# Four graph layers on one core: the first layer's pair loop takes its product of two row vectors from TensorE, and its epilogue no longer forms u

## The chip, the core and the metric

The kernel runs on one core of a Trainium2 chip. It computes four graph layers over 4096 nodes with 128 features each, in float32, in one launch. The metric is the device time of the launch in microseconds (us). Before the change it is 2199.0 us, the median of three runs (2198.42 to 2199.36).

An engine is named as the profile names it: PE is TensorE (PEld its weight loads), DVE is VectorE, ACT is ScalarE, POOL is GpSimd, SP is the queue that issues most transfers.

## The reference, cut to what matters

Only the first of the four layers is touched. For each node it makes a point h in the unit ball, and then sums, over the neighbours j of a node i, the logarithmic map of h_j seen from h_i, weighted by a sigmoid:

```python
        h = proj(mobius_add(mv, hyp_bias))                   # one 128-vector a node, |h| < 1
        x_tangent = logmap0(h)
        x_local = jax.vmap(lambda xi: logmap(xi, h))(h)      # for all 4096 x 4096 pairs
        logits = (x_tangent @ wl)[:, None] + (x_tangent @ wr)[None, :] + att_b[0]
        adj_att = adj * jax.nn.sigmoid(logits)
        support_t = jnp.einsum('ij,ijd->id', adj_att, x_local)
        h_agg = proj(expmap(h, support_t))
        out = proj(expmap0(proj_tan0(h_agg)))
        ...
    x = _layernorm(x + _L0_gnn_ref(x, adj, ...), axis=-1)
```

`logmap` is a multiple of a Moebius sum of the two points, times an inverse hyperbolic tangent of its norm. The kernel never forms it for a pair. With g = h / (1 - |h|^2) and e = sqrt(|g|^2 + 1/4) for each node, everything that a pair (i, j) needs is the scalar

    t = e_i * e_j - g_i . g_j

clamped from below just above 1/4, and a function phi(t) = ln(2 (2t + s)) / s with s = sqrt(4 t^2 - 1/4). The sums over j are then matrix products of (sigmoid x adj x phi) with g.

## The kernel before: the parts that the change and the steps touch

After a preamble that makes `H` (the g of all nodes, by rows), `HT` (the same, transposed), `gg` = |g|^2, `ex` = e, and the vectors of the sigmoid (`dl`, `dr`), comes the *pair loop*. It goes over the 36 pairs (I, J), I <= J, of the 8 x 8 blocks of 512 x 512 nodes. An off-diagonal pair does block (I, J) and block (J, I) at once (t is symmetric: the second one takes a transpose); 28 pairs are off-diagonal and 8 diagonal. Before the loop the rows e and dl are written to DRAM and read back, spread over all partitions:

```python
            ex = de[:, 1, :]
            nc.vector.tensor_scalar(ex, gg, 0.25, None, op0=ALU.add)
            nc.scalar.activation(ex, ex, AF.Sqrt)
            ...
            nc.tensor.transpose(p[0 : 2 * NT, 0, :], de.rearrange("p k t -> p (k t)"), self.ident)
            nc.scalar.copy(e2, p[0 : 2 * NT, 0, :])
            nc.sync.dma_start(out=rows.rearrange("k (t p) -> (k t) p", p=P), in_=e2)
```

The loop's operations, each for one pair `p` (and one block `m`, `b` or `ib` of 128 rows):

```python
            def load(p, k):                       # SP: broadcasts (di, ei or dj) and a 1 MB block of adj
                ...
                        row["d", I] = broadcast(0, I, "di")
                        row["e", I] = broadcast(1, I, "ei")
                ...
            def turn_adj(p, m):                   # PE: transposes a 128-row strip of adj into PSUM (2 buffers)
            def copy(p, m, put=nc.scalar.copy):   # ACT: takes it from PSUM into at
            def vcopy(p, m):                      # DVE: the same
            def store(p, k):                      # SP: writes the transposed block for the later layers, 1 MB
            def distance(p, b):                   # PE: pz = g_j . g_i for 128 x 512 pairs (PSUM, 2 buffers)
                nc.tensor.matmul(
                    pz, lhsT=HT[:, j * P : (j + 1) * P], rhs=HT[:, I * S : (I + 1) * S], start=True, stop=True
                )
            def shift(p, b):                      # DVE: t = e_i * e_j - pz
                nc.vector.scalar_tensor_tensor(
                    once(p, "t", wk, "t")[:, b, :], st[p]["e"], ex[:, j : j + 1], st[p].pop(("pz", b)),
                    op0=ALU.mult, op1=ALU.subtract,
                )
            def sigmoid(p, k):                    # ACT: 4 x sigmoid(d + dr), 128 x 512 each
            def mask(p, k):                       # DVE: w = w * at
            def clamp(p, _):                      # DVE: y = max(t, 0.25 + 5e-7)
                nc.vector.tensor_scalar(y, st[p]["t"], 0.25 + 5e-7, None, op0=ALU.max)
            def square(p, _):                     # ACT; then ln, root, inverse: ACT, all 128 x 2048
            def add_root(p, _):                   # DVE: t = 2 t + s
            def log(p, _):                        # ACT
            def phi(p, _):                        # DVE: t = t * y
            def first(p, _):                      # DVE: w0 = w0 * t
            def turn(p, ib):                      # PE: transposes t (the same 2 PSUM buffers as distance)
            def second(p, ib):                    # DVE: w1 = w1 * transposed t
            # sum_i, sum_j: PE, the two matrix products; add_j, add_i: DVE, adding them up in XA
```

The order of all these within a step is one string, `PAIR_ORDER`; the last number of an entry says how many pairs ahead of the step it works. An engine takes its instructions strictly in this order:

```python
PAIR_ORDER = """
turn_adj.4.0 first.0.-1 copy.4.0 distance.2.1 second.3.-1 mask.0.0 ln.0.0 turn_adj.1.1 turn.1.-1
root.0.0 sum_i.1.-2 turn_adj.0.1 shift.2.1 copy.1.1 copy.0.1 mask.1.0 load.1.1 add_i.0.-2 add_root.0.0
store.1.0 sum_j.0.-2 distance.1.1 turn_adj.3.1 turn_adj.5.1 inverse.0.0 sum_i.0.-1 second.1.-1
add_j.0.-2 distance.0.1 log.0.0 shift.1.1 sigmoid.0.1 vcopy.3.1 distance.3.1 turn_adj.2.1 add_j.1.-2
vcopy.5.1 sum_i.3.-1 phi.0.0 shift.0.1 load.0.2 turn_adj.7.1 sum_i.2.-1 copy.2.1 turn.2.0 shift.3.1
clamp.0.1 turn.0.0 turn_adj.6.1 vcopy.7.1 sigmoid.1.1 second.2.0 copy.6.1 second.0.0 square.0.1
sum_j.1.-1 store.0.1 turn.3.0
"""
```

The *epilogue* follows. `X` holds the weighted sums v of the 32 groups of 128 nodes. It forms u = bhalf v + sm g in place and sums its squares (`uu`), then w = sg u + b g and its squares (`wsq`), then c2 w + c1 b g and its squares (`gsq`), each a pass over 32 tiles of 128 x 128, with a few small column operations and activation-table loads between; then the residual and the layer norm, whose tiles go straight into the second layer:

```python
            for t in range(NT):
                nc.gpsimd.tensor_scalar(Hb[:, t, :], H[:, t, :], b[:, t : t + 1], None, op0=ALU.mult)
            for t in range(NT):
                nc.vector.scalar_tensor_tensor(           # gv = g . v
                    junk, H[:, t, :], 1.0, X[:, t, :], op0=ALU.mult, op1=ALU.mult, accum_out=gv[:, t : t + 1]
                )
                nc.scalar.activation(X[:, t, :], X[:, t, :], AF.Copy, scale=bhalf[:, t : t + 1])
            ...
            for t in range(NT):
                combine(t, sm, H, X, uu, 2)               # DVE: X = H * sm + X; its square on DVE or ACT
            un = self.norm("un", uu)
            th = self.act("sg", self.tt("unb", un, rb, ALU.mult), AF.Tanh)
            sg = self.tt("sgu", th, self.rec("run", un), ALU.mult)
            for t in range(NT):
                combine(t, sg, X, Hb, wsq, 2)             # DVE: X = X * sg + Hb; its square
            ...
            for t in range(NT):                           # Hb = Hb * c1, on POOL or ACT
                ...
            for t in range(NT):
                combine(t, c2, X, Hb, gsq, 3)             # DVE: X = X * c2 + Hb; its square
```

Of the kernel before, what the change touches and what calls it, by code (L numbers as in the profile page):

```python
# [9 lines left out]
F32 = mybir.dt.float32  # L10
# [22 lines left out]
turn_adj.4.0 first.0.-1 copy.4.0 distance.2.1 second.3.-1 mask.0.0 ln.0.0 turn_adj.1.1 turn.1.-1  # L33
root.0.0 sum_i.1.-2 turn_adj.0.1 shift.2.1 copy.1.1 copy.0.1 mask.1.0 load.1.1 add_i.0.-2 add_root.0.0
store.1.0 sum_j.0.-2 distance.1.1 turn_adj.3.1 turn_adj.5.1 inverse.0.0 sum_i.0.-1 second.1.-1
add_j.0.-2 distance.0.1 log.0.0 shift.1.1 sigmoid.0.1 vcopy.3.1 distance.3.1 turn_adj.2.1 add_j.1.-2
vcopy.5.1 sum_i.3.-1 phi.0.0 shift.0.1 load.0.2 turn_adj.7.1 sum_i.2.-1 copy.2.1 turn.2.0 shift.3.1
clamp.0.1 turn.0.0 turn_adj.6.1 vcopy.7.1 sigmoid.1.1 second.2.0 copy.6.1 second.0.0 square.0.1
sum_j.1.-1 store.0.1 turn.3.0
# [3 lines left out]
class Net:  # L43
# [234 lines left out]
    def layer0(self, x, weight, bias, att_w, att_b):  # L278
# [4 lines left out]
        with ExitStack() as ctx:  # L283
# [122 lines left out]
            de = self.cols.tile([P, 2, NT], F32, tag="de", name="de")  # L406
# [15 lines left out]
            ex = de[:, 1, :]  # L422
# [3 lines left out]
            nc.vector.reciprocal(b, rb)  # L426

# [7 lines left out]
            rows = self.dram.tile([2, N], F32, tag="rows", name="rows")  # L435
            p = self.ps_t.tile([P, 4, P], F32, tag="pt", name="pt")
            nc.tensor.transpose(p[0 : 2 * NT, 0, :], de.rearrange("p k t -> p (k t)"), self.ident)
            e2 = pre.tile([2 * NT, P], F32, tag="e2", name="e2")
            nc.scalar.copy(e2, p[0 : 2 * NT, 0, :])
            nc.sync.dma_start(out=rows.rearrange("k (t p) -> (k t) p", p=P), in_=e2)  # L440
# [8 lines left out]
            self.pair_loop(HT, HA, dr, ex, rows, adp, early)  # L449
# [5 lines left out]
            rot = ctx.enter_context(tc.tile_pool(name="rot0", bufs=4))  # L455
            Hb = late.tile([P, NT, D], F32, tag="Hb", name="Hb")
            gv = self.col("gv")
            for t in range(NT):
                nc.gpsimd.tensor_scalar(Hb[:, t, :], H[:, t, :], b[:, t : t + 1], None, op0=ALU.mult)
            for t in range(NT):  # L460
                junk = rot.tile([P, P], F32, tag="junk", name="junk")
                nc.vector.scalar_tensor_tensor(
                    junk, H[:, t, :], 1.0, X[:, t, :], op0=ALU.mult, op1=ALU.mult, accum_out=gv[:, t : t + 1]
                )
                nc.scalar.activation(X[:, t, :], X[:, t, :], AF.Copy, scale=bhalf[:, t : t + 1])
# [4 lines left out]
            def combine(t, a, src, add, sq, of_eight):  # L470

                k = slice(t, t + 1)
                junk = rot.tile([P, P], F32, tag="junk", name="junk")
                x = X[:, t, :]
                nc.vector.scalar_tensor_tensor(x, src[:, t, :], a[:, k], add[:, t, :], op0=ALU.mult, op1=ALU.add)
                if t * of_eight % 8 < of_eight:
                    nc.vector.scalar_tensor_tensor(
                        junk, x, 1.0, x, op0=ALU.mult, op1=ALU.mult, accum_out=sq[:, k]
                    )
                else:  # L480
                    nc.scalar.activation(junk, x, AF.Square, accum_out=sq[:, k])

            uu, wsq, gsq = self.col("uu"), self.col("wsq"), self.col("gsq")
            for t in range(NT):
                combine(t, sm, H, X, uu, 2)


            un = self.norm("un", uu)
            th = self.act("sg", self.tt("unb", un, rb, ALU.mult), AF.Tanh)
            sg = self.tt("sgu", th, self.rec("run", un), ALU.mult)  # L490
            for t in range(NT):
                combine(t, sg, X, Hb, wsq, 2)
# [8 lines left out]
            c1 = self.tt("c1", rden, wsq, ALU.mult)  # L501
            for t in range(NT):
                if t % 2:
                    nc.gpsimd.tensor_scalar(Hb[:, t, :], Hb[:, t, :], c1[:, t : t + 1], None, op0=ALU.mult)
                else:
                    nc.scalar.activation(Hb[:, t, :], Hb[:, t, :], AF.Copy, scale=c1[:, t : t + 1])
            for t in range(NT):
                combine(t, c2, X, Hb, gsq, 3)
# [10 lines left out]
            for t in range(NT):  # L519
                nc.vector.scalar_tensor_tensor(  # L520
                    X[:, t, :], X[:, t, :], gf[:, t : t + 1], x0[:, t, :], op0=ALU.mult, op1=ALU.add
# [4 lines left out]
    def pair_loop(self, HT, HA, dr, ex, rows, adp, early):  # L526
# [6 lines left out]
        with ExitStack() as ctx:  # L533
# [10 lines left out]
            row = {}  # L544
# [6 lines left out]
            def broadcast(k, I, tag):  # L551

                t = wk.tile([P, S], F32, tag=tag, name=tag)
# [9 lines left out]
            def load(p, k):  # L563
                I, J = pairs[p]
                if k == 0:
                    if I == J:
                        row["d", I] = broadcast(0, I, "di")
                        row["e", I] = broadcast(1, I, "ei")
                    else:
                        row["d", J] = broadcast(0, J, "dj")  # L570
                    st[p]["d"] = [row["d", i] for i, _ in sides(p)]
                    st[p]["e"] = row["e", I]
# [988 lines left out]
```

## Time and profile before

| stretch of the span (2194.8 us) | from - to, us | what it is |
|---|---|---|
| preamble | 0 - 71 | g, e and the sigmoid's vectors |
| pair loop | 71 - 766 | 36 pairs |
| epilogue of the first layer | 766 - about 842 | three passes, layer norm; the second layer's first products start at 842 |
| the other three layers | to 2194.8 | not touched |

The page gives the busy share of each engine over the whole span: PE 88%, DVE 86%, ACT 67%, POOL 4%. These are averages over stages with different limits, so the stages that the change touches are read for themselves. A stretch in the "windows" view has one column for each engine (busy us, and in brackets the number of instructions), then the granted TensorE clock, the mean busy share of the 16 transfer engines and the GB/s they moved. In the "lines" view a row is a group of instructions of one line of the kernel: engine, operation, output <- inputs, shape, count, then busy us in all and the mean ns of one, then how long the engine had been idle before them and for whom it waited. Consecutive instructions of one engine overlap a little in these records (the next one starts before the last one's record ends), so the sum of the means of a step is a little more than the step; the distance from one start to the next is the better cost where instructions follow each other without a wait.

### The profile page before, as it was taken

Reading aid. Unit: us, or ns where it says so; the run is one execution under the profiler, and the core shown is the slowest. Engines: PE = TensorE matmul, PEld = TensorE weight load, DVE = VectorE, ACT = ScalarE, POOL = GpSimd, SP = SyncE. Lnnn points to the kernel's source line nnn. Section 1 sums busy time; section 2 is a strip of 40 time slices with the busy share of each in tenths; the row PEclk is TensorE's granted clock in tenths of the full one; section 3 lists DMA queues with packets and bytes.
Section 4 is the critical chain, followed back from the end, with each engine's and each line's share of the span. In section 5 each row is a group of like instructions: output and inputs, shape, how many; then the busy total and the mean of one; then the engine's idle time right before and its main releaser. Section 6 shows DMA issues by size and latency. Waiting matters only on the chain.

```text
span 2194.8 us, 24059 instructions
## 1 busy us (share of the span) xinstructions
PE 1936.8 (88%) x8720; PEld 1043.1 (48%) x8720; DVE 1880.6 (86%) x2732; ACT 1474.8 (67%) x1858; POOL 97.8 (4%) x146
## 2 busy tenths in 40 slices
PE   5588888888888707999999999999997999999998
PEld 4366666666666604433333333333333444544443
DVE  6799999999999888789999999999998454568887
ACT  5799999999999774677787787787784122210000
POOL 2000000000000232210000000000000000000000
PEclk7699999999999957999999999999999999999999
DMA  3456566766666406994646465564554877767783
GB/s 94 138 205 232 199 229 211 244 211 229 208 204 211 147 1 223 227 241 166 198 173 186 159 194 185 181 189 173 174 207 187 318 267 269 267 249 278 292 297 112
DMA packets 112868, 448.44 MB, mean 204 GB/s; under 512 B 9760, under 2 KB 20064, under 8 KB 71776
## 3 DMA queue, kind: packets, MB, share of 16 engines
q1 hardware_dynamic: 94160, 361.82, 46.8%
q10 hardware_dynamic: 9360, 68.16, 9.1%
q0 software_dynamic: 9216, 16.78, 4.3%
q8 instruction: 73, 1.20, 0.2%
q14 instruction: 59, 0.48, 0.1%
HBM read 369.10 MB, written 77.63 MB: 204 GB/s over the span
## 4 chain that ended last, share of the span: by engine, by line
PE 41%; DVE 35%; ACT 17%; issue 5%; DMA 2%; POOL 0%; ACTq 0%; SPq 0%; DVEq 0%; POOLq 0%
PE pa L1264 10%; PE pv L926 9%; DVE e L909 9%; PE pa L1444 9%; PE ps L900 6%; ACT e L907 4%; DVE w L620 4%; ACT w L612 3%; DVE t L603 2%; DVE nat L890 2%; DVE w L652 2%; DVE t L648 2%; DVE w L663 2%; DVE at L584 1%; DVE t L640 1%
## 5 line engine op out<-in xcount | busy, mean ns | idle before, releaser
L909 DVE SCALAR_TENSOR_TENSOR e<-at,e 128x2048 f32<-128x2048 f32 x256 | 582.8, 2286 | 69.5 <-ACT e L907 68.9
L907 ACT ACTIVATE e<-ps 128x1024 f32<-128x1024 f32 x512 | 493.1, 1024 | 146.2 <-PE ps L900 126.3
L926 PE MATMUL pv<-e,VA 128*64 128x512 f32 x2048 | 495.8, 605 | 6.6 <-DVE e L909 4.9
L900 PE MATMUL ps<-QS,KS 128*128 128x512 f32 x1024 | 313.4, 425 | 4.9 <-ACT e L907 2.6
L900 PEld LDWEIGHTS ps<-QS,KS 128*128 128x128 f32 x1024 | 171.7, 189 | 229.5 <-ACT e L907 174.4
L926 PEld LDWEIGHTS pv<-e,VA 128*64 128x64 f32 x2048 | 124.6, 136 | 249.4 <-issue 215.1
L1264 PE MATMUL pa<-ring,Y 128*128 128x512 f32 x512 | 225.7, 594 | 0.0
L580 PE MATMUL ptA<-ident,ad 128*128 128x128 f32 x1024 | 159.5, 285 | 51.6 <-ACT at L584 48.1
L1444 PE MATMUL pa<-w,F 128*128 128x512 f32 x448 | 195.3, 594 | 0.0
L580 PEld LDWEIGHTS ptA<-ident,ad 128*128 128x128 f32 x1024 | 120.7, 145 | 132.5 <-ACT at L584 95.8
L1441 DVE SCALAR_TENSOR_TENSOR w<-rho,col,ring 128x512 f32<-128x512 f32 x224 | 162.7, 745 | 22.9 <-PE pa L1444 10.3
L596 PE MATMUL pz<-HT 128*128 128x512 f32 x288 | 152.8, 633 | 23.3 <-DVE w L663 16.2
L675 PE MATMUL pi<-HA,w 128*128 128x129 f32 x1152 | 153.6, 278 | 0.6 <-DVE w L652 0.6
L1264 PEld LDWEIGHTS pa<-ring,Y 128*128 128x128 f32 x512 | 95.9, 191 | 111.5 <-issue 111.3
L620 DVE TENSOR_TENSOR w<-w,at 128x2048 f32<-128x2048 f32 x64 | 146.0, 2282 | 0.5 <-ACT at L584 0.5
L675 PEld LDWEIGHTS pi<-HA,w 128*128 128x128 f32 x1152 | 141.4, 194 | 3.8 <-issue 2.3
L1444 PEld LDWEIGHTS pa<-w,F 128*128 128x128 f32 x448 | 83.7, 190 | 106.1 <-issue 78.3
L881 ACT ACTIVATE nat<-nat 128x2048 f32<-128x2048 f32 x64 | 122.6, 1916 | 3.7 <-DMA nat<-in_adj_dram 3.6
L690 PE MATMUL pj<-HA,w 128*128 128x129 f32 x896 | 109.5, 274 | 3.0 <-DVE w L663 3.0
L603 DVE SCALAR_TENSOR_TENSOR t<-ei,de,pz 128x512 f32<-128x512 f32 x144 | 103.6, 738 | 9.5 <-DMA ei<-rows 7.0
L690 PEld LDWEIGHTS pj<-HA,w 128*128 128x128 f32 x896 | 104.5, 191 | 3.2 <-DVE w L663 3.2
L658 PE MATMUL ptz<-ident,t 128*128 128x128 f32 x448 | 70.0, 282 | 33.8 <-DVE w L663 24.7
(359 smaller groups left out, 2446.5 us busy)
## 6 DMA issues: line engine op xcount, KB each, us to landing
ring<-adjT SPq DMA_DIRECT2D x128, 1024.0 KB, 4.8
ad<-in_adj_dram SPq DMA_DIRECT2D x64, 1024.0 KB, 5.3
adjT<-at SPq DMA_DIRECT2D x64, 1024.0 KB, 5.0
nat<-in_adj_dram ACTq DMA_DIRECT2D x64, 1024.0 KB, 5.0
at<-adjT SPq DMA_DIRECT2D x63, 1024.0 KB, 4.8
qk<-cut SPq DMA_DIRECT2D x16, 512.0 KB, 12.1
KS<-qk POOLq DMA_DIRECT2D x32, 256.0 KB, 7.4
QS<-qk POOLq DMA_DIRECT2D x32, 256.0 KB, 5.6
```

What stands on the lines that cost most here:

```text
L580: nc.tensor.transpose(pt[:, ib, :], ad[:, ib, jb * P : (jb + 1) * P], self.ident)
L596: nc.tensor.matmul(pz, lhsT=HT[:, j * P : (j + 1) * P], rhs=HT[:, I * S : (I + 1) * S], start=True, stop=True)
L620: nc.vector.tensor_tensor(w, w, st[p][f"at{k}"], ALU.mult)
L675: nc.tensor.matmul(row[I, "po"][ib // 2][:, ib % 2, :], lhsT=st[p]["w0"][:, jb, ib * P : (ib + 1) * P], rhs=HA[:, 4 * J + jb, :], start=False,
L690: nc.tensor.matmul(pj[:, a, :], lhsT=st[p]["w1"][:, ib, jb * P : (jb + 1) * P], rhs=HA[:, 4 * I + ib, :], start=(ib == 0), stop=(ib == 3),)
L900: nc.tensor.matmul(p[:, h, :], lhsT=KS[:, h2 + h, jb * P : (jb + 1) * P], rhs=QS[I % 2][:, h2 + h, :], start=True, stop=True,)
L907: nc.scalar.activation(e[:, h2 : h2 + 2, :], p, AF.Exp)
L909: nc.vector.scalar_tensor_tensor(e, at[:, jb % 4, :].unsqueeze(1).to_broadcast([P, NH, S]), 0.0, e, op0=ALU.not_equal, op1=ALU.mult,)
L926: nc.tensor.matmul(st["po"][h // 2][g : g + 64, :], lhsT=VA[:, o : o + 64], rhs=e[:, h, :], start=(jb == 0), stop=(jb == NT - 1), skip_gro ...
L1264: nc.tensor.matmul(st["pa"], lhsT=Y[:, 4 * J + jb, :], rhs=at[:, jb, :], start=False, stop=(J == NS - 1 and jb == 3), skip_group_check=True,)
L1441: nc.vector.scalar_tensor_tensor(w, rho[:, I * S : (I + 1) * S], col[:, 0, j : j + 1], at[:, jb, :], op0=ALU.max, op1=ALU.mult)
L1444: nc.tensor.matmul(pa, lhsT=F[:, j, :], rhs=w, start=False, stop=(j == NT - 1), skip_group_check=True)
```

## The change

Three things change, all in the first layer.

1. **The product e_i e_j moves to TensorE.** e is cut into two parts that together carry it (a float32r part, and the rest, again in float32r); the products of the parts, with a minus sign, are added to pz by a second matmul with a contraction of only 4 rows. `shift` becomes one operation with two constants, which negates and clamps at once, so `clamp` is gone, and the broadcast row `ei` with it. The parts come from DRAM by POOL's queue, for each pair (`el`) and each row of blocks (`er`).

```diff
@@ distance
-                    pz, lhsT=HT[:, j * P : (j + 1) * P], rhs=HT[:, I * S : (I + 1) * S], start=True, stop=True
+                    pz, lhsT=HT[:, j * P : (j + 1) * P], rhs=HT[:, I * S : (I + 1) * S], start=True, stop=False
+                )
+                nc.tensor.matmul(
+                    pz, lhsT=st[p]["el"][:, b * P : (b + 1) * P], rhs=row["er", I], start=False, stop=True
                 )
@@ shift
-                nc.vector.scalar_tensor_tensor(
-                    once(p, "t", wk, "t")[:, b, :], st[p]["e"], ex[:, j : j + 1], st[p].pop(("pz", b)),
-                    op0=ALU.mult, op1=ALU.subtract,
+                nc.vector.tensor_scalar(
+                    once(p, "t", wk, "t")[:, b, :], st[p].pop(("pz", b)), -1.0, 0.25 + 5e-7, op0=ALU.mult, op1=ALU.max
                 )
-            def clamp(p, _):
-                y = once(p, "y", wk, "y", bufs=1)
-                nc.vector.tensor_scalar(y, st[p]["t"], 0.25 + 5e-7, None, op0=ALU.max)
@@ vectors(p), called at the start of each step for the pair two ahead
+                        er = row["er", I] = wk.tile([4, S], F32R, tag="er", name="er", bufs=2)
+                        for k in range(2):
+                            nc.gpsimd.dma_start(out=er[2 * k : 2 * k + 2, :], in_=rows[1:3, I * S : (I + 1) * S])
+                el = st[p]["el"] = wk.tile([4, S], F32R, tag="el", name="el", bufs=3)
+                for k in range(2):
+                    nc.gpsimd.dma_start(
+                        out=el[2 * k : 2 * k + 2, :], in_=rows[3 + k, J * S : (J + 1) * S].partition_broadcast(2)
+                    )
```

   The order of a step is new. `distance` and `shift` now run two pairs ahead, the chain from `square` to `phi` one pair ahead. Four of the eight strips of an off-diagonal pair's adj are now taken from PSUM by DVE and four by ACT (before: three and five), two and two of a diagonal pair's four (before: one and three). The natural-log table is loaded when the first of its functions comes, instead of after the last sigmoid:

```diff
-turn_adj.4.0 first.0.-1 copy.4.0 distance.2.1 second.3.-1 mask.0.0 ln.0.0 turn_adj.1.1 turn.1.-1
  ... (the rest of the order before stands above)
+mask.1.0 sigmoid.0.2 turn.2.0 load.1.1 square.0.1 turn_adj.0.1 sum_j.1.-1 second.0.0 second.2.0
+vcopy.0.1 turn.1.0 second.1.0 ln.0.1 turn_adj.6.1 add_j.0.-2 root.0.1 turn.3.0 store.1.0 turn_adj.2.1
+add_i.0.-1 distance.3.2 second.3.0 vcopy.6.1 copy.2.1 distance.2.2 turn_adj.3.1 load.0.2 first.0.0
+sum_j.0.-1 shift.3.2 copy.3.1 turn_adj.5.1 inverse.0.1 shift.2.2 turn_adj.7.1 store.0.1 add_root.0.1
+mask.0.1 vcopy.7.1 distance.0.2 sum_i.2.0 copy.5.1 log.0.1 turn_adj.4.1 shift.0.2 phi.0.1 distance.1.2
+shift.1.2 sum_i.3.0 sigmoid.1.1 turn_adj.1.2 sum_i.0.0 sum_i.1.0 turn.0.1 copy.4.1 add_j.1.-1 vcopy.1.2
```

2. **The parts of the first two pairs are made on the chip**, in the preamble, by small column operations, transposes and copies (`rows4`), so that they need no trip through DRAM. The row of the sigmoid still makes that trip, now after one more step of the preamble:

```diff
+            for k in range(2):
+                part = self.cols.tile([P, NT], F32R, tag="part", name="part")
+                nc.vector.tensor_copy(part, ex)
+                nc.vector.tensor_copy(de[:, 1 + k, :], part.bitcast(F32))
+                if k == 0:
+                    nc.vector.tensor_tensor(ex, ex, de[:, 1, :], ALU.subtract)
  ... (12 small copies into cols4)
+            for k in range(3):
+                p = self.ps_t.tile([P, 4, P], F32, tag="pt", name="pt")
+                for t in range(4):
+                    nc.tensor.transpose(p[0:4, t, :], cols4[:, k, t, :], self.ident)
+                self.evacuate(rows4[k], p[0:4, :, :].rearrange("p a b -> p (a b)"))
```

3. **The epilogue does not form u.** |u|^2 is a quadratic form in the columns |g|^2, g.v and |v|^2, so one pass over the tiles goes; w is made from v and g at once. The scaled part of each sum is made tile by tile on ACT (five of eight) or POOL (three of eight):

```diff
             for t in range(NT):
                 ...                                        (gv = g . v on DVE, as before)
-                nc.scalar.activation(X[:, t, :], X[:, t, :], AF.Copy, scale=bhalf[:, t : t + 1])
+                nc.scalar.activation(junk, X[:, t, :], AF.Square, accum_out=vv[:, k])
-            for t in range(NT):
-                combine(t, sm, H, X, uu, 2)
-            un = self.norm("un", uu)
+            un = self.norm("un", quadratic("uu", sm, bhalf))
+            wg, wv = self.tt("wg", sg, sm, ALU.mult), self.tt("wv", sg, bhalf, ALU.mult)
+            nc.vector.tensor_tensor(wg, wg, b, ALU.add)
             for t in range(NT):
-                combine(t, sg, X, Hb, wsq, 2)
+                scaled(t, part, X[:, t, :], wv[:, k])
+                nc.vector.scalar_tensor_tensor(w[:, t, :], H[:, t, :], wg[:, k], part, op0=ALU.mult, op1=ALU.add)
+                if t % 4 == 3:  ...                        (square and its sum on DVE)
+                else:
+                    nc.scalar.activation(junk, w[:, t, :], AF.Square, accum_out=wsq[:, k])
  ... (the third pass likewise: part = c1 b g, then w = c2 w + part, then the squares, again one in four on DVE)
```

## The prediction

> **What bounds the kernel now.** I first cut the span into stages with the windows view. In the pair loop both elementwise engines are full and TensorE is not; columns after the stretch: its length, then busy us of PE, PEld, DVE, ACT, POOL, the granted clock, DMA share and GB/s.
>
> ```profile
> 71.00:115.00 44.00, 30.23 (x94) 17.53 (x95) 30.20 (x29) 37.83 (x37) 0.00 (x0) 0.69 0.53 174
> ...
> 155.00:194.80 39.80, 34.62 (x245) 27.61 (x244) 39.73 (x40) 39.39 (x41) 0.00 (x0) 1.00 0.63 225
> ...
> 234.00:750.00 516.00, 437.10 (x2975) 343.77 (x2974) 509.85 (x482) 512.09 (x514) 0.00 (x0) 0.99 0.63 215
> ```
>
> DVE and ACT are 99% busy from 115 us on, PE 85%. The critical chain through two steps gives the period: the phi product of consecutive off-diagonal pairs begins 19.75 us apart (columns: start, us, what).
>
> ```profile
> 155.29 2.20 DVE t L648
> ...
> 175.04 2.20 DVE t L648
> ...
> 194.79 2.20 DVE t L648
> ```
>
> Then the lines view, kept apart by shape, over exactly one such step (155.21 to 174.96 us): the operations that the change touches, with their mean ns.
>
> ```profile
> L603 DVE SCALAR_TENSOR_TENSOR t<-ei,de,pz 128x512 f32<-128x512 f32 x4 | 2.9, 738 | 0.0
> L584 ACT COPY at<-ptA 128x512 f32<-128x512 f32 x5 | 2.8, 576 | 0.0
> L584 DVE COPY at<-ptA 128x512 f32<-128x512 f32 x4 | 2.7, 680 | 0.0
> ...
> L612 ACT ACT_TABLE_LOAD x2 | 2.6, 1283 | 0.0
> ...
> L624 DVE TENSOR_SCALAR y<-t 128x2048 f32<-128x2048 f32 x1 | 1.2, 1227 | 0.0
> ```
>
> (The window's edges catch a fourth DVE copy; a step has three.) From start to next start in the timeline, without overlap, a clamp costs 1.14 us, a shift 0.66, a DVE copy from PSUM 0.60, an ACT copy 0.475, a full 128x2048 product 2.20. Added up, a step is 19.7 us on DVE (two masks 4.4, shifts 2.65, clamp 1.14, add_root, phi and first 6.6, second 2.4, copies 1.8, add_j 0.66) and 19.46 on ACT (its sigmoids 5.05, five copies 2.4, square, ln, root, inverse, log 9.4, two table loads 2.6). So DVE sets the period, with ACT 0.3 us behind it.
>
> In the epilogue the timeline shows three passes with a norm between:
>
> ```profile
> 774.66 0.67 DVE L475 SCALAR_TENSOR_TENSOR X<-HA,sm,X 128x128 f32<-128x128 f32 x2
> ...
> 785.78 1.28 ACT L239 ACT_TABLE_LOAD   x1
> ...
> 789.16 0.62 DVE L475 SCALAR_TENSOR_TENSOR X<-X,sgu,Hb 128x128 f32<-128x128 f32 x2
> ...
> 801.28 10.63 POOL L504 TENSOR_SCALAR Hb<-Hb,c 128x128 f32<-128x128 f32 x16 [23.41 <-DVE c L226]
> ...
> 814.48 1.28 ACT L239 ACT_TABLE_LOAD   x1
> ```
>
> u takes 774.7 to 785.8, its norm 3.4 us, w 789.2 to 799.9, the third pass 801.2 to 814.5.
>
> **What the skill says.** "VectorE: DVE Perf Modes", section "The perf-mode tier table", has a float32 tensor_scalar at twice the rate of a two-input operation, but not from PSUM. The trace agrees: the clamp, 2048 columns from SBUF, took 1227 ns against 2282 for a mask, while a copy of 512 columns from PSUM took 680. I therefore charge the new shift, single-input from PSUM, like that copy: folding the clamp in costs nothing. "TensorE: Matmul & The Clock Gate", section "LDWEIGHTS", says that a weight load costs by its columns, not by the contraction depth; so 4 rows won't make the small matmul cheap. No run here shows a 4-row one. The nearest row is the second layer's float32r product of the same 512 columns with 128 rows, at 0.28 us from start to start in a run of four.
>
> **The change part by part.**
>
> Loop, DVE: -1.14 (clamp), -4 x 0.06 (shift 0.66 to 0.60), +0.60 (a fourth copy from PSUM): 19.7 becomes 18.9. Loop, ACT: -0.475 (a copy less): 19.46 becomes 18.98. The table loads stay two a step: in the new order the second sigmoid of one step and the first of the next stand together, with only a copy and then square near them, and the four log and exp operations stand together too. So ACT now sets the period, 19.0 us, and DVE is within 0.1 of it. Off-diagonal pairs: 28 x (19.75 - 19.0) = 21 us. A diagonal pair is ACT's anyway, one copy less: 8 x 0.475 = 4. Gross 25.
>
> Loop, PE: start to start, a step has 12 sets of four transposes at 0.44, four distances at 0.86, 16 + 16 products (two records each) at 0.22: 15.9 us. Four small matmuls add 4 x 0.28 = 1.1: 17.0 of 19.0. Not the bound by sum. I walked the new order by hand with these costs. With ACT's step starting at 0, root ends at 9.5, add_root runs 9.5 to 11.7, log needs it at 12.7; log ends at 14.65, phi needs it at 15.1; the last copy ends at 18.97 and the next step's mask waits for just that. On PE, the PSUM buffers come free in time but for one: the transpose after sum_j waits about 0.8 us for ACT's copy at 10.0; PE still closes its step near 18.2. So the period of 19.0 is feasible, with some 1 us of play on each link.
>
> Transfers: 1 MB stores land in 5.0 us (median; 8.2 at most), loads in 5.3. The tight one is the store of the second block: it starts after the last copy of a step, and DVE writes into its buffer 5.5 us into the next. If it lands late, DVE slips behind ACT by up to 1 us without cost, which covers 6.5 us, not 8.2. I charge 0.1 us a step: 4 us. The el and er transfers have three and two buffers and can be issued two steps ahead, so 7.4 us to landing (the like transfers of the second layer) is hidden.
>
> Start of the loop: before, e is ready at 70.15, rows goes out at 70.95, di is asked for at 72.80 and the first sigmoid starts at 77.36. Now five dependent column operations (0.22 each) make the parts, and the transposes of the 12 small columns may come before that of the rows: 1.5 to 5 us later, so the first sigmoid at 79 to 83. The shifts no longer wait (6.98 us for ei before), but the shift isn't ACT's bound. ACT's earlier copies (74 to 77) are no longer done while it waits. ACT had 671 us of work between 71 and 755.3, the end of the last log. Now 671 - 36 x 0.475 = 654. From 81 on, with 4 us of losses: 739. The tail (phi, first, sum_i, add_i, 10.7 us) stays. The loop therefore ends about 16 us earlier. The gross 25 shrinks because before, too, ACT's own work was 8 us less than the period (28 x 0.3), and because of the later start.
>
> Epilogue: first pass, 32 ACT squares with their sums at 0.295 = 9.4 us, just as the 9.46 us of scalings now. Then the quadratic form's last links, 3 x 0.22 us, instead of the pass of 10 us: -9.5. Three new column operations: +0.5. Second pass, ACT: 20 scalings + 24 squares at 0.295 = 13 us against 10.7 now, where DVE set it (DVE has 32 x 0.27 + 8 x 0.29 = 11, POOL 12 x 0.73 = 9): +2.5. Third pass: ACT 13 against 13.3: 0. The lead of a tile over three engines: +1 in all. Sum -5.5.
>
> Total: 2199 - 16 - 5.5 = 2177.5; I take 2178.
>
> **The rivals.**
>
> First, PE becomes the bound. For: it is at 85% already, its waits are for PSUM buffers (its weight loads waited 58.1 us for ACT's copies between 200 and 650 us), there are two buffers for each kind, and every distance now holds one for 0.28 us longer. If the small matmul cost the 0.42 us of its mean record, and a switch of type more, PE would need 17.6 to 18.5. Against: its sum stays below 19.0. If it is right, the period stays at 19.5 to 19.8 and the loop gains 0 to 7: 2185 to 2195.
>
> Second, a new wait on a transfer takes the place: DVE on the store (above), or ACT on di, which is now asked for only after the store in the middle of the step before. For: SP takes its transfers in order, and landing reaches 8 to 9 us at most. Against: medians of 5.0 and 6.3 fit. If it is right, 0.3 to 0.5 us a step is lost: 2184 to 2190.
>
> Third, the gain is all there and the new order does better than I charge (no losses, the sigmoid at 79, the epilogue at -9): 2168.
>
> **Range and chances.** The centre is ACT's sum with small losses. The largest doubt is the coupling of three engines within 1 us of each other, which can only cost; I give it up to 12 us. The start and the epilogue are each good to 3 us. So 2166 to 2193. A gain of over 2% needs 2155, more than even the lossless sum gives: 0.05. Over 2% slower needs 1.8 us more a step, which would take a broken prefetch: 0.02. Within 2%: 0.93.
>
> **What would show it.** Right: phi to phi 19.0 us, ACT at 99% and DVE just below in the loop, PE at 89 to 91% (17.0 of 19.0), shift near 680 ns, the small matmul near 0.28 us apart, still 72 table loads in the loop, the first sigmoid at 79 to 83, the loop's end near 750, and from there to the second layer's first product about 5 us less than the 76 us of before. Wrong: idle time of DVE before copies from PSUM that ends on a store; ACT idle before its copies that ends on a PE transpose; el landing late; or shift at 740 ns, which would make DVE the bound again at 19.2.

## The result and the profile after

| | us (median, lowest to highest) | against the kernel before |
|---|---|---|
| before | 2199.2 (2198.4 to 2200.3) | |
| after | 2184.1 (2182.2 to 2184.5) | 0.9929, 95% interval 0.9912 to 0.9946 |

15.1 us less, and within the range predicted (2166 to 2193); the centre was 6 us too low. First the same stretches of the windows view of the changed kernel (columns as before: length, busy us of PE, PEld, DVE, ACT, POOL, granted clock, DMA share, GB/s):

```profile
71.00:115.00 44.00, 33.22 (x92) 15.38 (x93) 23.75 (x39) 34.80 (x41) 3.31 (x6) 0.68 0.25 73
...
157.41:195.90 38.49, 37.45 (x251) 28.93 (x251) 38.07 (x40) 37.88 (x39) 3.08 (x6) 1.00 0.68 238
234.38:747.74 513.36, 484.56 (x3099) 362.85 (x3099) 497.57 (x488) 504.22 (x490) 31.81 (x62) 0.99 0.64 220
```

In two full steps (second line) PE is busy for 97% of the time, where 89 to 91% was predicted; DVE has 99%, ACT 98%. Three engines are now nearly full at once. The chain that ends the two steps gives the period (phi is L714):

```profile
157.49 2.20 DVE t L714
...
161.23 2.21 DVE w L686
163.44 0.03 issue
163.47 0.02 DVEq L729
163.49 0.04 issue
163.53 1.29 DVE w L729 x2
...
176.74 2.15 DVE t L714
...
195.98 2.08 DVE t L714
```

Phi to phi is 19.25 and 19.24 us, not 19.0, and the whole chain is DVE. Between the mask (L686) and the next `second` (L729) it holds 0.09 us in which nothing runs, with an entry of DVE's own sequencer (DVEq) in the middle. The mask takes 2.20 us from its start to the next when work follows directly; here it takes 2.30 in the chain, and 2.39 from record to record, since the records no longer overlap either. The same stands between `first` and the next shift (2.39 again). Now the lines view by shape over one step (176.65 to 195.90):

```profile
L666 DVE TENSOR_SCALAR t<-pz 128x512 f32<-128x512 f32 x5 | 3.3, 685 | 0.1
...
L660 PE MATMUL pz<-rows,el 4*128 4x512 f32 x4 | 2.0, 492 | 0.0
...
L674 ACT ACT_TABLE_LOAD x1 | 1.3, 1283 | 0.0
...
L660 PEld LDWEIGHTS pz<-rows,el 4*128 4x128 f32 x4 | 0.7, 182 | 3.0 <-issue 3.0
```

The shift has its 685 ns (680 predicted), and the tables are still loaded twice a step (the other load is at `ln`). The last line is the one to stop at: the weight loads of the 4-row matmul were idle for 3.0 us, 0.76 before each, and waited for nothing that the profile shows. They start only when the distance before them has run out. The timeline of PE and of its weight loads (PEld) shows what that costs (columns: start, length, then the instruction, and in brackets how long the engine was idle before it):

```profile
167.54 1.12 PE L657 MATMUL pz<-HT 128*128 128x512 f32 x2
168.60 0.49 PE L660 MATMUL pz<-rows,el 4*128 4x512 f32 x1
...
168.60 0.18 PEld L660 LDWEIGHTS pz<-rows,el 4*128 4x128 f32 x1 [0.76 <-issue]
...
169.02 0.66 PE L641 MATMUL ptA<-ident,ad 128*128 128x128 f32 x4
```

The small matmul takes 0.42 us from its start to the next one, and the distance before it is longer too: 1.06 here. Over the four pairs of the step that begins at 176.65 the distance and the small matmul take 5.69 us from start to start; four distances of one step of a kernel without the small matmul (below) take 3.61. So one costs (5.69 - 3.61) / 4 = 0.52 us, not 0.28, and four make PE's step 15.9 + 2.1 = 18.0 us, not 17.0.

Last the epilogue, in the timeline:

```profile
758.08 0.28 DVE L505 SCALAR_TENSOR_TENSOR junk<-HA,X 128x128 f32<-128x128 f32 x1
...
767.14 1.28 ACT L238 ACT_TABLE_LOAD   x1
...
771.70 1.62 DVE L524 SCALAR_TENSOR_TENSOR w<-HA,wg,part 128x128 f32<-128x128 f32 x5 [0.52 <-POOL part L498]
...
787.24 1.62 DVE L548 SCALAR_TENSOR_TENSOR w<-w,c,part 128x128 f32<-128x128 f32 x5 [0.80 <-POOL part L498]
...
827.86 2.04 PE L865 MATMUL pqk<-XT,wk 128*128 128x512 f32 x2
```

The loop ends at 758.1 instead of 766.0 (-8); from there to the second layer's first product are 69.8 us instead of 76 (-6). The table load of the norm of u stands 9.1 us after the loop's end, where it stood at 785.78, 19.8 us after it: the pass that made u is gone.

### The profile page after: what moved, and what is told of

It reads as the page before. It is cut to its first block, busy times and chain, and to the rows that moved or that the text cites. A ratio compares the mean times of both kernels' runs of the same rounds, so it can differ in the third digit from the quotient of the medians.

```text
span 2182.5 us, 24442 instructions
## 1 busy us (share of the span) xinstructions
PE 2000.2 (92%) x8876; PEld 1066.8 (49%) x8876; DVE 1849.3 (85%) x2700; ACT 1458.3 (67%) x1847; POOL 120.4 (6%) x204
## 4 chain that ended last, share of the span: by engine, by line
PE 43%; DVE 31%; ACT 16%; DMA 5%; issue 4%; SPq 0%; POOL 0%; ACTq 0%; DVEq 0%; POOLq 0%
PE pa L1332 10%; PE pv L994 10%; PE pa L1512 9%; DVE e L977 8%; PE ps L968 6%; ACT e L975 4%; DVE w L686 3%; DMA adjT<-at 2%; ACT w L674 2%; DVE nat L958 2%; DVE w L718 2%; DVE t L705 2%; DVE w L729 2%; DVE t L666 2%; DVE at L645 2%
## 5 line engine op out<-in xcount | busy, mean ns | idle before, releaser
L641 PE MATMUL ptA<-ident,ad 128*128 128x128 f32 x1024 | 154.0, 280 | 16.2 <-DMA ad<-in_adj_dram 9.4
L657 PE MATMUL pz<-HT 128*128 128x512 f32 x288 | 159.8, 638 | 1.5 <-DVE e L463 0.9
L686 DVE TENSOR_TENSOR w<-w,at 128x2048 f32<-128x2048 f32 x64 | 146.3, 2285 | 0.0
L666 DVE TENSOR_SCALAR t<-pz 128x512 f32<-128x512 f32 x144 | 96.1, 686 | 16.5 <-PE pz L660 12.8
L645 DVE COPY at<-ptA 128x512 f32<-128x512 f32 x128 | 87.2, 686 | 11.9 <-PE ptA L641 7.1
```

What stands on the lines that cost most here:

```text
L641: nc.tensor.transpose(pt[:, ib, :], ad[:, ib, jb * P : (jb + 1) * P], self.ident)
L657: nc.tensor.matmul(pz, lhsT=HT[:, j * P : (j + 1) * P], rhs=HT[:, I * S : (I + 1) * S], start=True, stop=False)
L686: nc.vector.tensor_tensor(w, w, st[p][f"at{k}"], ALU.mult)
```

## The experiments

Theory A after the reading: DVE's chain with its two gaps sets the period of 19.24, and PE at 97% only stands beside it. Theory B: PE has become the bound (the first rival). Times are to be held against 2184.1 for the changed kernel; "first phi" and "last phi" are read in the timeline (94.4 and 755.3 before, 100.6 and 747.7 after).

**The small matmul left out.** The product e_i e_j isn't added, so the output lacks it.

```diff
-                nc.tensor.matmul(pz, lhsT=st[p]["el"][:, ...], rhs=row["er", I], start=False, stop=True)
```

> Leaves the second, 4-row matmul out of every distance (the product of the two e is then missing from t). Theory A, the period of 19.24 us in the loop is VectorE's own chain of work, with two gaps of 0.19 us where an instruction waits for the one just before it: the period stays at 19.15 to 19.25, TensorE's busy time in a step falls by about 2.4 us (4 x 0.61), and the whole gains only what the start gains, 0 to 4 us against the changed kernel. Theory B, TensorE at 97% sets the period through its two PSUM buffers: the period falls to ScalarE's 18.95, and the whole by 8 us or more.

Measured: 2179.9 us in one run. Between 200 and 650 us (windows view):

```profile
200.00:650.00 450.00, 392.49 (x2663) 316.61 (x2661) 438.41 (x434) 443.58 (x435) 0.00 (x0) 0.98 0.63 220
```

PE falls to 392 of 450 (428 with it), and full steps still take 19.23 to 19.24. PE isn't what sets the period. The few us gained lie at the start: first phi at 97.3, 3.3 earlier; last phi at 743.7, 4.0 earlier. From first to last phi it is 646.4 us, against 647.1 in the changed kernel: in this run the room that PE got did not shorten the loop. One thing besides PE's work differs: nothing reads el and er, so POOL issues their transfers ahead (0.00 us of POOL in this line, 29.8 with the small matmul).

**The small matmul twice** (the product is added twice):

```diff
+                nc.tensor.matmul(pz, lhsT=st[p]["el"][:, ...], rhs=row["er", I], start=False, stop=False)
                 nc.tensor.matmul(pz, lhsT=st[p]["el"][:, ...], rhs=row["er", I], start=False, stop=True)
```

> Issues the 4-row matmul twice in every distance. It prices the small matmul. If 0.28 us is its true cost when the one before it is of the same type, TensorE's step grows from 18.6 to 19.7 us; if it costs 0.42 whatever stands before it, to 20.25. The period must follow, since TensorE then needs more than 19.24: 19.8 to 20.5 us, the whole 15 to 40 us longer. Theory A and B agree here; if the period stays below 19.4, TensorE has far more play than its busy time shows and B is out.

Measured: 2197.2 in one run, 13 us above the changed kernel and a little under the 15 to 40 expected; full steps of 19.24 to 20.8; PE 442 of 450. PE's timeline, the second small matmul and what follows it:

```profile
232.00 0.39 PE L663 MATMUL pz<-er,el 4*128 4x512 f32 x1
232.32 1.13 PE L657 MATMUL pz<-HT 128*128 128x512 f32 x2
```

The second one costs only 0.31 to 0.34 us from start to start, and its weight load, which starts at 231.76 while the first one runs, is hidden. So it isn't the small matmul as such that is dear: what remains is the step from 128 rows to 4 or the change of type, on either side of it. PE has little room beyond this one more.

**The small matmul in float32**, so that it has the type of the distance:

```diff
-  rows4, er, el: [4, S], F32R
+  rows4, er, el: [4, S], F32
```

> The same four rows, but held and multiplied as float32 instead of float32r. In the trace the weight load of the float32r matmul begins only when the float32 matmul before it is done (0.76 us idle before it), and the load after it waits likewise. If the change of type is what costs, the small matmul falls from 0.61 us (0.42 and 0.19 more for the one before) to about 0.43 in a step of two float32 passes, and TensorE's step from 18.6 to about 17.9. Theory A: the period stays at 19.2 and the time within 2 us of the changed kernel (2182 to 2186). Theory B: the period falls to 18.95 and the time to 2174 to 2178. If the type is not what costs, TensorE's step grows and so does the time.

Measured: 2245.4 (2240.2 to 2247.8), ratio 1.0218 (1.0201 to 1.0235), full steps of 20.77, PE 447 of 450. It now costs 1.05 us, and the weight load is still idle for 0.76 before it, and as long before the next 128-row load. With the type the same on both sides the load still isn't hidden, so the change of type was not the cause. And this is what a loop looks like in which PE is busy for 99% of the time.

**DVE's two gaps filled.** Two `add_j` are moved to where DVE would otherwise wait for its own last instruction:

```diff
-mask.1.0 sigmoid.0.2 ...      first.0.0 sum_j.0.-1 shift.3.2 ...
+mask.1.0 add_j.0.-2 sigmoid.0.2 ...      first.0.0 add_j.1.-1 sum_j.0.-1 shift.3.2 ...
```

> Only the order: the two small additions of sum_j's result are moved to stand between mask and the first second, and between first and the first shift, where VectorE waits for its own previous instruction (mask to second 2.39 us instead of 2.20, first to shift the same). Theory A: each gap of 0.19 goes, the period falls from 19.24 to 18.9 to 19.0 (ScalarE's sum), the time by 5 to 9 us to 2175 to 2179. Theory B: no change, period 19.2, time 2182 to 2186.

Measured: 2182.1 (2178.7 to 2188.2), ratio 0.9930 (0.9907 to 0.9953): by time no difference from the changed kernel, and short of the 2175 to 2179 expected. But the gap is gone (timeline of DVE; the mask and what follows it),

```profile
180.68 2.28 DVE L686 TENSOR_TENSOR w<-w,at 128x2048 f32<-128x2048 f32 x1
182.88 0.41 DVE L768 COPY X<-pj 128x258 f32<-128x258 f32 x1
```

2.20 us, and undisturbed steps take 18.85 to 18.88. Theory A holds for the period, and fell short for the time: first to last phi is 646.8 us against 647.1. The first three steps took 59.2 us instead of 56.8 (granted clock 0.56 between 97 and 116 us, 0.82 in the changed kernel), and several later ones grew to 19.5 to 20.1. The waits view of this kernel, 160 to 740 us (us in total, times, longest), names on what:

```profile
DVE at L645 <- PE ptA L641: 8.0, 6, 2.4
DVE at L645 <- DMA adjT<-at: 4.4, 8, 0.9
```

It is 3.8 and 3.1 us in the changed kernel. I read it so: PE turns the blocks late, so DVE and ACT copy late and the stores start late. That reading is argued, not shown; whether it hangs on PE's missing slack or on the transfers themselves was open.

**The transfers spread.** In the spaced order the load of a pair's second block is issued at the end of the step before:

```diff
-turn.2.0 load.1.1 square.0.1 ...      turn_adj.4.1 shift.0.2 ...
+turn.2.0 square.0.1 ...      turn_adj.4.1 load.1.2 shift.0.2 ...
```

> The spaced order, and in it the load of the second block is issued some 6 us earlier, at the end of the step before, so that it no longer shares the start of a step with the store. Theory: what the spaced order gained by its period of 18.85 was given back in waits for the store and for blocks that were not yet transposed; with the transfers spread these waits shrink, and first phi to last phi falls from 646.8 to 637 to 642 us, total 2173 to 2178. Rival: what was given back hangs on the coupling of the engines or on di and dj, and the loop stays at 645 to 648, total 2181 to 2183.

Measured: 2207.3 (2197.6 to 2215.9), ratio 1.0035 (1.0018 to 1.0052): worse than both expectations. The waits view of ACT, same stretch:

```profile
ACT w L674 <- DMA di<-rows: 23.1, 7, 4.4
```

It was 2.9 us in the spaced order and 1.9 in the changed kernel. SP issues its transfers in the order of the program, and the load now stands ahead of di: in the step that begins at 212.06, di goes out at 211.21, right behind the early load (210.78) and 0.9 us before the phi; in the spaced order it goes out 4.7 us before it (210.34 and 215.00). Seven steps of 21 to 22.6 us came with it, six of them with a granted clock of 0.84 to 0.95 in their windows.

**The small operands padded to 128 rows** with zeros, written once; the transfers still fill rows 0 to 3, and the output is the same:

```diff
-  rows4 (3), el (3 buffers), er (2 buffers): [4, S]
+  8 tiles [P, S], memset to 0 at the start
```

> The changed kernel with the small operands padded to 128 rows with zeros (the tiles are zeroed once at the start, the transfers fill rows 0 to 3), so that the small float32r matmul has as many rows as its neighbours; the output is the same. Theory R (the change of the number of rows is what keeps the weight load from being hidden): start to start near 0.28 us, no 0.76 us of idle weight loading before it, the distance before it back to 0.86, PE busy between 200 and 650 us about 419 of 450 instead of 428; the period stays 19.24 because DVE sets it; the start gains some 1 to 3 us: 2181 to 2184. Rival F (the change of type from float32 to float32r costs it): still about 0.6 us for each, PE busy 428, time as the changed kernel.

Measured: 2178.1 (2175.5 to 2181.2), ratio 0.9902 (0.9884 to 0.9920); its range and that of the changed kernel don't touch. PE's timeline:

```profile
162.44 1.02 PE L659 MATMUL pz<-HT 128*128 128x512 f32 x2
162.90 0.79 PE L662 MATMUL pz<-rows,rows 128*128 128x512 f32 x1
...
162.88 0.19 PEld L662 LDWEIGHTS pz<-rows,rows 128*128 128x128 f32 x1 [0.24 <-issue]
...
163.53 0.60 PE L643 MATMUL ptA<-ident,ad 128*128 128x128 f32 x4
```

The weight load now starts at 162.88, while the record of the distance runs on to 163.46, and is idle for 0.24 us before instead of 0.76. Distance and small matmul together 1.09 us instead of 1.48; over the four of a step 4.45 instead of 5.69: with 32 times the rows one costs (4.45 - 3.61) / 4 = 0.21 us instead of 0.52. PE is busy for 408 of 450. Full steps still take 19.23 (DVE's gaps are still there), and DVE no longer waits for a store in the list of its waits between 160 and 740 us. Theory R holds: the change of the number of rows was dear, not the type. The total is 3 us below the 2181 to 2184 expected. Of the 9.1 us by which the last phi comes earlier in the profiles (738.7, 747.7 in the changed kernel), 4.8 are there by the fourth phi (152.6, 157.4).

This kernel also begins differently. Granted clock (third column from the end) and PE's busy time at the start, first of the changed kernel,

```profile
81.00:86.00 5.00, 5.00 (x7) 1.57 (x6) 1.38 (x2) 4.91 (x8) 2.47 (x5) 0.50 0.07 17
86.00:91.00 5.00, 5.00 (x16) 3.10 (x15) 2.08 (x3) 2.65 (x3) 0.00 (x0) 0.50 0.01 2
```

and of the padded one:

```profile
81.00:86.00 5.00, 4.49 (x25) 3.01 (x23) 3.09 (x5) 5.00 (x8) 1.19 (x3) 1.00 0.03 5
86.00:91.00 5.00, 2.06 (x6) 0.76 (x4) 0.18 (x1) 4.94 (x4) 0.00 (x0) 1.00 0.00 0
```

With four rows PE is busy for the whole 10 us, and at half clock; a distance with its small matmul takes 2.73 us there, and the square of the first pair waits for the fourth of them until 88.4. With 128 rows the clock is full from 81 on, the square starts at 84.65, and the first phi comes at 96.8.

**Only the first two pairs padded**, to part the start from the loop:

```diff
-  rows4 (3): [4, S];  rhs=row["er", I]
+  rows4 (3): [P, S], zeroed;  rhs=row["er", I] if p < 2 or I else rows4[0][0:4, :]
```

> Only the parts of the first two pairs, those made on the chip, are padded to 128 rows; all later pairs keep four rows. Theory: two gains of the padded kernel are separate. At the start the granted clock reaches 1.0 before 81 us instead of 91 and the first phi comes at 96.5 to 97.5 instead of 100.6; in the loop nothing changes against the changed kernel (first phi to last phi 645 to 649, PE busy between 200 and 650 us near 428), total 2179 to 2182. Rival: the clock at the start has another cause than the rows of the matmuls (the order in which things arrive differs a little from run to run): it stays at 0.5 to 90, first phi at 100 to 101, total 2183 to 2186.

Measured: 2183.3 (2180.7 to 2186.8), ratio 0.9931 (0.9911 to 0.9951). The clock is 0.80 from 76 to 81 and 1.00 from 81 to 91, first phi at 97.0, as the theory says. The gain then goes: PE waits 8.2 us for a load of adj (7.9 in the padded kernel), and with four-row pairs after it the clock is 0.50 on average from 97 to 116 and 0.80 from 116 to 141 (1.00 in the padded kernel's steps after 113); the third step takes 24.7 us, and the fourth phi comes at 159.5 (157.4 in the changed kernel). So the total misses the expectation by 1 to 4 us, and padding the first two pairs alone is not shown to pay. From the fourth phi on, this loop of four-row pairs takes 587.8 us (590.3 in the changed kernel, 586.1 in the padded one), so what the padding gains there is not much more than what profiles of one loop differ by.

**Both edits**, the spaced order and the padding:

> Both edits at once: the spaced order (two add_j moved into the two places where DVE waits for its own last instruction) and the small operands padded to 128 rows. Theory: the spaced order alone gave its period of 18.85 back because PE, near full, turned the blocks late and so the stores started late; with PE's slack back the period holds in most steps, first phi to last phi falls from 641.8 (padded) to 630 to 637 us, total 2166 to 2174. Rival: what was given back doesn't hang on PE (transfers alone): steps of 19.5 and more stay, loop 640 to 643, total 2176 to 2180.

Measured: 2176.1 (2175.4 to 2176.9), ratio 0.9890 (0.9874 to 0.9907). First to last phi 640.2 us, at the rival's end of what was expected: the period is 18.85 in undisturbed steps, but few are undisturbed. PE waited 12.9 us for loads of adj (1.9 in the padded kernel), one step took 20.65. It is the fastest of the twelve, though its range lies within the padded one's but for 0.1 us. With the padding, filling the gaps is worth 2 us in the medians, and that is not clear of noise.

**The parts of the first pairs by transfers too**, without the small columns and transposes:

```diff
-  cols4, rows4; st[p]["el"] = rows4[1 + p] for p < 2; row["er", 0] = rows4[0]
+  el and er of every pair by the two dma_start each
```

> The changed kernel, but the first pairs' parts come by transfers like those of all other pairs; no small columns, no transposes on the chip. Theory: e's rows go out some 2.5 us earlier and the first sigmoid with them (78 to 79), but the first distance waits for el and er (two steps of some 5 us after the rows), at 80 or later instead of 76.7, and PE is still at a low clock then: square of pair 0 at 91 to 93 instead of 88.4, total 2186 to 2189. Rival: the sigmoids set the start, then it begins earlier: first phi at 98, total 2181 to 2183.

Measured: 2188.7 (2184.7 to 2192.4), ratio 0.9954 (0.9935 to 0.9972). The total is as the theory said, but not for its reason: the first sigmoid starts at 76.7 instead of 81.1, the square at 87.9 instead of 88.4, and the first phi comes at 100.1 instead of 100.6. The first small matmul waits for el until 78.2, and then the half clock sets the pace as before. The intervals of the two kernels overlap, and this one's profile has a span of 2182.8, like the changed kernel's 2182.5. A gain from making the parts on the chip is not shown.

**The order of before** for the changed operations (its clamp dropped):

> The changed kernel with the order of operations of before (only the clamp dropped from it): ACT still makes five of the eight copies and DVE three. Theory: ACT, 19.46 us of work a step, sets the period then: phi to phi 19.5 to 19.7 in full steps, so nearly all of the loop's gain needs the fourth copy on DVE, and the total is 2189 to 2194. Rival: the order matters little and dropping the clamp alone gives the gain: period 19.2 to 19.3, 2182 to 2186.

Measured: 2217.3 (2216.9 to 2219.3), ratio 1.0081 (1.0064 to 1.0097). The period in full steps is 19.39, ACT's sum with five copies, near what the theory had (19.46). The time is 23 us beyond it. A full step and one of three long ones, in the windows view:

```profile
187.96:207.34 19.38, 18.55 (x125) 14.23 (x124) 18.34 (x19) 19.29 (x21) 1.03 (x2) 1.00 0.69 232
414.61:438.83 24.22, 21.93 (x94) 14.94 (x92) 17.97 (x17) 18.98 (x21) 2.05 (x4) 0.73 0.55 185
```

In the long steps the granted clock is 0.70 to 0.73 while PE is busy for 91% of the step; ACT waits 5 to 7 us in each for blocks that PE turns. The new order, with its fourth copy on DVE, is worth some 33 us with four-row matmuls in the loop. Why the clock falls just there wasn't tried.

**The parts of the gain.** The kernel before with the new epilogue alone:

> The pair loop and the start of the kernel before, with only the new epilogue (u not formed). Theory: the epilogue's gain is its own and simply adds: from the loop's end to the second layer's first product 69.8 us as in the changed kernel instead of 76.0, loop as before (phi to phi 19.75, last phi near 755.3), total 2199 - 6 = 2193 (2191 to 2194). Rival: the epilogue hides behind something the second layer waits for anyway, and the time stays at 2197 to 2199.

2192.6 (2191.3 to 2194.2), ratio 0.9966 (0.9952 to 0.9980): -6.6 us. And the new start and loop with the epilogue of before:

> The changed start and pair loop, with the epilogue of before. Theory: the loop ends 8 us earlier as in the changed kernel (last phi near 747.7), then 76 us of epilogue: total 2199 - 8.5 = 2190.5 (2188 to 2192), and the two parts add up to the 15 us of the whole. Rival: the parts don't add (a part of the epilogue's gain is won only with the new loop, or the other way round), then the two gains together differ from 15 by more than 4 us.

2195.0 (2190.1 to 2203.6), ratio 0.9979 (0.9971 to 0.9988): -4.3 us, and above the 2188 to 2192 expected. By the medians the two make 10.9 us of the 15.1, which is 4.2 less and just past the 4 us that the expectation had set for "the parts don't add"; by the ratios they make 0.9945, at the edge of the whole's interval (0.9912 to 0.9946). Whether the parts add stays open; the loop's share is the uncertain one, 4 to 9 us. Its fourth to last phi takes 594.3 us here, 590.3 in the changed kernel and 590.8 with the parts by transfers, with the same loop in all three: its waits for transfers and the clock vary by a few us.

## Why the prediction was right, and where its terms were off

- **The epilogue**: -5.5 predicted, -6.2 in the profile and -6.6 by itself. By links: to the table load of the norm 10.7 us less (-9.5 charged), from there to the second pass 1.2 more (+0.5), from the second to the third pass 3.4 more (+2.5, and +1 for the lead of a tile), the rest equal. The sum over links was right within a us or so each.
- **The shift, the clamp, the table loads, the hidden transfers of el**: as predicted (685 ns; 72 loads in the loop; PE never waited for el in the loop).
- **The start**: the first sigmoid came at 81.1, in the middle of 79 to 83. But the step "the shift isn't ACT's bound" fell: ACT waited 2.3 us for the fourth shift before the first square, since the distances ran at half clock. The first phi is 6.3 us later than before; by the fourth, 2.2 are left.
- **The period**: "ACT now sets the period, 19.0 us, and DVE is within 0.1 of it" was wrong by 0.24. DVE's sum of 18.9 counted 2.20 us for each full product, which holds only where the next instruction doesn't wait for the last one of its own engine. In two places of the new order it does, 0.19 us each: 18.85 + 2 x 0.19 = 19.23. Over 28 pairs that is 6.7 us, nearly the difference between the 16 us predicted for the loop and the 8 measured. That sum is tempting and isn't the whole answer: with the gaps filled the time stayed within 2 us.
- **The losses**: "From 81 on, with 4 us of losses: 739" is the term of the total that was off most. The windows view from ACT's first sigmoid to the end of its last log, first of the changed kernel and then of the padded one (ACT is the fourth engine):

```profile
81.09:747.57 666.48, 623.74 (x3901) 460.64 (x3901) 634.38 (x619) 651.85 (x635) 41.39 (x81) 0.98 0.63 216
79.73:738.48 658.75, 578.38 (x3896) 468.79 (x3895) 632.20 (x619) 650.72 (x635) 41.50 (x81) 0.99 0.63 219
```

ACT has the work that was predicted (651.9 us, 654 charged), but loses 14.6 us and not 4; that is why the loop ends at 758 and not at 750. The padded kernel loses 8.0, the one without the small matmul 11.9, the spaced one 15.3, the one with both edits 7.1, each in one profile. So the padding goes with smaller losses; what makes up the rest is open.
- **The price of the small matmul** was off too: 4 x 0.28 = 1.1 us a step on PE were charged, and 4 x 0.52 = 2.1 measured. The Trainium skill's page "TensorE: Matmul & The Clock Gate", section "LDWEIGHTS", led me to expect the same cost for 4 rows as for 128, and for the load itself that holds (182 ns against 190). Not priced was that the load isn't hidden. The same page, section "Step-by-step: what each phase is for", says that a load is pulled ahead of running matmuls when the row groups don't conflict or when it goes to the background buffer. Here a load of another row count isn't pulled ahead, while the second of two with 4 rows is. Padded to the rows of its neighbours, the matmul costs 0.21 us and the kernel takes 2178.1. That this is the predicted centre is in part luck: its full steps take 19.23 us and not 19.0, and its 4 us of losses beyond those charged are made up by an earlier first sigmoid (79.7) and 3 us less of work.
- **The rivals**: "PE becomes the bound" is refuted for the period (19.24 without the small matmul too), though its estimate of 17.6 to 18.5 us of PE a step was the true one. What I take it to have done instead is take the slack: 97% busy, PE passes late transfers and dips of the clock on to DVE and ACT. The smaller losses of the padded kernel and its missing waits for stores speak for that; the run without the small matmul, where PE has the most room and the loop is no shorter, speaks against it. It is not shown. The second rival, waits on stores and on di, happened at a small scale (DVE 3.1 us for stores, ACT 1.9 for di between 160 and 740 us; stores land in 6.1 us, 5.0 before), about the 4 us charged. The third, no losses at all, did not come.

## What to carry to other kernels

Price a small matmul inside a stream of full ones by what it does to its neighbours' weight loads, and try it padded with zeros to their row count: here that took its cost from 0.52 to 0.21 us and 6 us off the whole, part of it at the start of the loop. When several engines are within a few per cent of the period, shortening the one that ends the chain can buy little: 0.38 us a step became 2 us in all. And in a hand-made order, don't put an instruction directly behind the one of its own engine that it has to wait for.

## What the runs showed of the hardware

- A change from 128 to 4 rows between matmuls, in either direction, keeps the next weight load from being hidden: a float32r matmul of 512 columns cost 0.52 us between full ones, 0.31 to 0.34 behind one of its own kind, and 0.21 with 128 rows; in float32 the 4-row one took 1.05.
- The granted clock at the loop's start stayed at 0.50 until 86 us or later in the eight kernels that began with four-row matmuls (the changed one, the two spaced ones without padding, the doubled one, the float32 one, the one with parts by transfers, the one with the order of before, the loop alone), though PE's records are busy from 81 to 91 without a gap. It was full from 81 us on in the three with 128-row ones at the start and in the one with none. The Trainium skill's page "TensorE: Matmul & The Clock Gate", section "What's actually happening", says that the clock is released by how busy PE was, after one window of about 3.4 us. Here, in the changed kernel, 10 us of busy records (5.00 of 5.00 twice, at 0.50) were not enough. Padding the first two pairs alone brought the full clock by 81, so it hangs on the rows of these matmuls; whether few rows count for less, or the time of the unhidden loads doesn't count, was not tried.
- A DVE instruction directly behind the one of its own engine that it waits for started 0.19 us later than one that doesn't wait (2.39 us instead of 2.20 after a 128x2048 product).
